# Another pace for expert tiles beside the last convolutions and the last mixing, and the last image's norms with both halves together

## The chip, the cores and the metric

The kernel runs on one core of a Trainium2 chip. The metric is the device time of one execution in microseconds, given as the median of three runs. A profiled execution of the same program is used to see where the time goes. Its engines are TensorE (PE, whose weight loads are listed apart as PEld), VectorE (DVE), ScalarE (ACT), GpSimd (POOL) and SyncE (SP, which here mostly issues DMA transfers).

## The reference

Four images of 256 channels and 32 x 32 positions pass through one layer: a token mixer with a residual, and then a mixture of experts with a residual. Cut to what matters here:

```python
def mixer(xs):                                   # xs: tokens of one image, 1024 x 256
    xn = layernorm(xs, norm_w, norm_b)
    xm = mamba_v(xn in 4 groups of 64 channels) + skip * xn       # selective scans
    g  = sigmoid(conv1d(conv1d(xm, qdw), qpw));  xg = g * xm
    R  = conv1d(conv1d(xg, rdw), rpw) + xg
    xm2 = conv1d(conv1d([xs, R], fdw), fpw) + xs                  # "convolutions"
    x_local  = conv1d(xm2, lc)
    x_global = mha(xm2)                                           # "attention"
    x_out = gelu(layernorm([x_local, x_global] @ fc_w.T + fc_b, lgn_w, lgn_b))
    xi = conv2d_depthwise_3x3(ln_hw(x_out), dwc)                  # "taps"
    return layernorm(xi, norm_w, norm_b) @ proj_w.T + proj_b      # "mixing" ends here

x = x + mixer(ln_c(x))
t = tokens(x);  xf = ln_t(t)
top_w, top_i = top_k(xf @ Wg + bg, 2);  w = softmax(top_w)        # "routing", 8 experts
for e in range(8):
    out += w_of_e * (gelu(xf @ W1[e] + b1[e]) @ W2[e] + b2[e])    # "expert tiles"
return t + out
```

Everything is float32. Each of the 4096 tokens goes to two experts of 256 x 1024 and 1024 x 256 weights.

## The kernel before

An image is held as two chunks of 128 channels by 1024 tokens, and most products and norms work on a half of 512 tokens at a time (`h` in the names). The images are staggered. While the selective scan of one image runs, pieces of its neighbours are put between its steps: convolutions, attention, mixing and routing of earlier images, and the first norm of later ones. After the last scan (image 3, `b == B - 1`) there is a tail of three stages and a fourth of tiles alone:

- the last convolutions (`convolutions(B - 1)`), beside which run the taps, the last norm, the projection and the routing of image 2 (`around(B - 2)`, `sent_off(B - 2)`);
- the last attention (`attention(B - 1)`);
- the last mixing: `joined(B - 1)` (output product `ao`, product `fc`, first norm `lgn`, gelu), `around(B - 1)` (norm over positions, then two times eight taps on DVE into `xi`), `sent_off(B - 1)` (mean, second norm `fin`, projection `pr`, then the routing in `experts.dispatch`);
- expert tiles alone, and the way back of the output.

**The experts.** `dispatch` computes gates (`gate`), places (`places`) and scatters each token's row by sixteen indirect DMAs on POOL's queue into `XS`, one region per expert. For the last image it also writes eight blank blocks behind the regions (`blank_ends`, L1457, issued from ACT's queue at L1450). A *tile* is 256 rows of one expert. There are 39, in three series of 8, 8 and 23. A series can start when enough images have been routed: `experts.series` (L1709) then makes on DVE a table of which tile belongs to which expert, and SP reads the table to address the loads. One tile loads two halves of W1 and two of W2 (512 KB each), two biases and its rows `xs` (L1786), and then runs, by the tile's instructions in their order:

- `xp` (L1832): four transposes of the rows on PE, copied by DVE to `xT`, and four small DVE operations;
- `h` 0 to 3 (L1855): four groups of matmuls, each with two gelus on ACT into `hs` (L1860);
- `y` (L1865): sixteen matmuls in four groups (k 0 to 3 and 4 to 7, for two row halves), which read `hs`; then `ys` on DVE (L1870, L1875) and two indirect DMAs on POOL that add into `Y`.

The next tile's loads, rows and `xp` are issued between the groups of the tile that runs.

**The order of the work** is written out by the program itself. Under `tc.manual_schedule` every engine executes its instructions in the order in which the Python code issues them. The pieces are generators; a `beat()` raises a tick, and a generator that yields `n` is resumed `n` ticks later. The tile generator (`tiles()`, L1148) yields `T["pace",]` after each of its eight groups of matmuls, or 1 if no pace is set. A pace above 1 spreads the groups of a tile over more steps of the other pieces, a pace below 1 packs them. `PACE` (L1273) holds a pace for each part of the last mixing, and `pace(b, ticks)` sets it, for the last image alone. There is none for the last convolutions. When these are done, `hold` stops the tiles at the next tile's start until two steps before the last attention ends.

**Norms.** `inverse_deviation` (L1000) makes the squares of a half on ACT, their mean over the channels on PE (`var`, L371), and the root as exp of -0.5 ln on ACT (`root`, L352); first for one half, then for the other. Then DVE multiplies both channel chunks. Gelu, sigmoid and the pair ln and exp belong to different tables of ACT; `loaded[0]` keeps track, and an ACT_TABLE_LOAD is issued at each change.

PSUM is one pool of eight banks (`ps`). Activations live in pools of tiles of 8, 4 and 2 KB per partition; the weights of the tiles reuse the buffers of the scan steps (`dts`, `dt`), enough for two tiles.

Of the kernel before, what the change touches and what calls it, by code (L numbers as in the profile page):

```python
# [72 lines left out]
def network(  # L73
# [29 lines left out]
    B = x.shape[0]  # L103
# [25 lines left out]
    eps5 = cpool.tile([P, 1], F32, name="eps5")  # L129
# [14 lines left out]
    with tc.tile_pool(name="w_conv", bufs=1) as wp, tc.tile_pool(  # L144
        name="act8", bufs=8
    ) as act8, tc.tile_pool(name="act4", bufs=7) as act4, tc.tile_pool(
        name="act2", bufs=17
    ) as act2, tc.tile_pool(name="steps", bufs=2) as actd, tc.tile_pool(
        name="steps4", bufs=6
    ) as acts, tc.tile_pool(name="rows", bufs=3) as actc, tc.tile_pool(  # L150
        name="small", bufs=1
# [190 lines left out]
        def half(h):  # L342
            return ts(h, HALF)
# [8 lines left out]
        def root(r, var, eps, scale=1.0):  # L352

            log_exp()
            nc.scalar.activation(r, var, AF.Ln, bias=eps, scale=scale)
            nc.scalar.activation(r, r, AF.Exp, scale=-0.5)
# [10 lines left out]
        def column_mean(name, chunks):  # L367

            out = ps(name)
            for ci, chunk in enumerate(chunks):  # L370
                nc.tensor.matmul(  # L371
                    out, ones_mean, chunk, start=(ci == 0), stop=(ci == len(chunks) - 1)
                )
            return out
# [110 lines left out]
        T = {}  # L485
# [511 lines left out]
            if b == B - 1:  # L997
                T["pace",] = ticks

        def inverse_deviation(name, xc):  # L1000
            r = a4(f"r_{name}")

            def squares(h):
                sq = [a2(f"sq_{name}_{h}_{c}") for c in range(NC2)]
                for c in range(NC2):
                    nc.scalar.activation(sq[c], xc[:, c, half(h)], AF.Square)
                return sq

            for h in range(2):
                sq = squares(h)  # L1010
                yield 1
                var = column_mean(f"var_{name}_{h}", sq)
                yield 2
                root(r[:, half(h)], var, eps5)
                yield 1
            yield 1
            for c in range(NC2):
                nc.vector.tensor_tensor(xc[:, c, :], xc[:, c, :], r, ALU.mult)
                yield 1

        def joined(b):

            xloc, oT = XLOC.pop(b), OT.pop(b)
            pace(b, PACE["product"])
            xglo = a8(f"xglo_{b}")
            T["attending", b] = True
            yield from in_turn(
                CO_H, lambda at: product(
                    f"ao_{b}_{at[0]}_{at[1]}", aoutT_s, at[0],
                    [oT[ci][:, half(at[1])] for ci in range(NC2)],  # L1030
                ),
                lambda at, r: nc.scalar.activation(
                    xglo[:, at[0], half(at[1])], r, AF.Identity, bias=ob[:, at[0] : at[0] + 1]
                ),
            )

            xc = XC[b] = a8(f"xc_{b}")
            both = (xloc, xglo)
            yield from in_turn(
                CO_H, lambda at: product(  # L1040
                    f"fc_{b}_{at[0]}_{at[1]}", fcT_s, at[0],
                    [both[ci // 2][:, ci % 2, half(at[1])] for ci in range(4)],
                ),
                lambda at, r: nc.scalar.activation(
                    xc[:, at[0], half(at[1])], r, AF.Identity, bias=fcb[:, at[0] : at[0] + 1]
                ),
            )

            T["joining", b] = True
            pace(b, PACE["norm"])  # L1050
            yield from inverse_deviation(f"lgn_{b}", xc)
            for c in range(NC2):
                nc.scalar.activation(
                    xc[:, c, :], xc[:, c, :], AF.Gelu, bias=col("lgn_b", c), scale=col("lgn_w", c)
                )
            loaded[0] = None
            log_exp()
            yield 2
# [44 lines left out]
        def sent_off(b):  # L1103

            xc = XC.pop(b)

            def centre(h, mean):
                for c in range(NC2):
                    nc.vector.tensor_tensor(
                        xc[:, c, half(h)], xc[:, c, half(h)], mean, ALU.subtract  # L1110
                    )

            pace(b, PACE["norm"])
            xr = a8(f"xr_{b}")
            nc.sync.dma_start(xr, x[b].rearrange("(c p) n -> p c n", p=P))
            yield from in_turn(
                range(2),
                lambda h: column_mean(f"mean_{b}_{h}", [xc[:, c, half(h)] for c in range(NC2)]),
                centre,
            )  # L1120
            yield from inverse_deviation(f"fin_{b}", xc)

            def residual(at, r):
                co, h = at
                inner = xr[:, co, half(h)]
                nc.vector.scalar_tensor_tensor(
                    inner, r, prb[:, co : co + 1], inner, ALU.add, ALU.add
                )

            yield from in_turn(  # L1130
                CO_H, lambda at: product(
                    f"pr_{b}_{at[0]}_{at[1]}", projT_s, at[0],
                    [xc[:, ci, half(at[1])] for ci in range(NC2)],
                ), residual,
            )
            pace(b, PACE["routing"])
            for ticks in experts.dispatch(
                b, xr, act8.tile(experts.XR, F32, tag="a8", name=f"XR_{b}"), root,
                log_exp,
            ):  # L1140
                if experts.counted == b:
                    pace(b, PACE["rows"])
                yield ticks
            T["sent", b] = True
            pace(b, 1)
# [118 lines left out]
        def until(*flag):  # L1264
            while not T.get(flag):
                beat()
# [3 lines left out]

        PARTS = 2 * NB

        PACE = {"product": 4, "norm": 2.2, "taps": 0.9, "routing": 2, "rows": 0.75}  # L1273
        with tc.manual_schedule(engines=ALL):
            log_exp()
            start(weights(), first_normalised())
            drain()
            first_part()
            for b in range(B):
                for p in range(PARTS):  # L1280
                    at = b * PARTS + p
                    stop = b > 0 and p == PARTS // 2 - 1 or at == len(parts) - 1
                    if b == 0 and p == 0:
                        start(later_weights())
                    if b == 0 and p == 2:
                        start(normalised(1))
                    if b > 0 and p == 0:
                        start(convolutions(b - 1))
                    if at == len(parts) - 1:
                        start(tiles())  # L1290
                    for i in range(NSTEP):
                        scan(at, i, stop)
                        if b > 0 and p == 0 and i == 9:
                            whole(b - 1)
                        beat()
                    if b > 0 and p == PARTS // 2 - 1:
                        drain()
                        start(
                            one_by_one(attention(b - 1), joined(b - 1)), finish_part(at),
                            one_by_one(  # L1300
                                local(b - 1), *([around(b - 2)] if b > 1 else []),
                                *([normalised(b + 1)] if 1 < b < B - 1 else []),
                            ),
                        )
                        if b > 1:
                            flag = "attending" if b == B - 1 else "joining"
                            start(behind_flag((flag, b - 1), sent_off(b - 2)))
                        if b == 1:
                            start(normalised(b + 1))
                        while not T.get(("attended", b - 1)):  # L1310
                            beat()
                        resume(at + 1)
            T["scanned",] = True
            start(
                flagged(finish_part(len(parts) - 1), "whole", B - 1),
                flagged(convolutions(B - 1), "convolved"),
                one_by_one(around(B - 2), sent_off(B - 2)),
            )
            until("convolved")
            T["hold",] = True  # L1320
            until("held")
            start(flagged(attention(B - 1), "attended", B - 1, 2), local(B - 1))
            until("attended", B - 1, 2)
            T["hold",] = False
            start(one_by_one(joined(B - 1), around(B - 1), sent_off(B - 1)))
            drain()

# [24 lines left out]
class Experts:  # L1352
# [11 lines left out]
    T = 256  # L1364
# [649 lines left out]
```

## Time and profile before

| | |
|---|---|
| three runs | 2481.73, 2473.77, 2473.78 us |
| median | 2473.78 us |
| profiled execution | 2480.27 us, of which the span from first to last instruction 2478.30 us |
| PE busy | 2131.6 us (86% of the span), 8810 matmuls |
| DVE busy | 1631.0 us (66%) |
| ACT busy | 1196.3 us (48%) |
| POOL busy | 1101.3 us (44%) |
| mean granted PE clock | 0.909 |
| DMA | 244.31 MB, mean 99 GB/s |

The busy shares are averages over the whole span. Up to about 1664 us the scans run, and DVE is busy for 1372 of these 1664 us; the tail behind it takes the remaining 815 us. In this part the page's row of the granted clock, in tenths over 40 slices, reads 7 to 9, and 9 in most slices of the tail.

Some ways of reading are needed later. In the timeline a line gives the start, the length from the first to the last of the merged instructions, engine, source line, operation, and in brackets the idle time before it with the instruction that ended it. PE counts each float32 matmul as two, so a group of four in the code is `x8` there. Matmuls overlap, so the difference of two starts, not the length, is the cost of a group. The granted clock is 1.00 where PE may run at full speed.

### The profile page before, as it was taken

The page shows a single profiled execution, that of the slowest core. Times are in us where ns is not written, and L with a number is a line of the kernel's source. Part 1 is how long each engine was busy: PE and PEld are TensorE (multiplying, and loading weights), DVE is VectorE, ACT ScalarE, POOL GpSimd, SP SyncE. Part 2 cuts the span into 40 slices and gives each one's busy share as a digit, 9 for nine tenths or more (in the row PEclk, how much of TensorE's full clock was granted, in tenths as well). Part 3 has the DMA queues.
Part 4 walks back from the last instruction along what each step waited for, and adds up shares of the span by engine and source line. Part 5 has one row for each costly group of instructions (what it writes and reads, how often), then busy time and mean ns, then how long its engine had stood idle before and what let it go on. Part 6 is the DMA issues. An engine that isn't in the chain of part 4 may idle for free. (4 is left out here: it accounts for less than half of the span.)

```text
span 2478.3 us, 28314 instructions
## 1 busy us (share of the span) xinstructions
PE 2131.6 (86%) x8810; PEld 947.8 (38%) x8810; DVE 1631.0 (66%) x2255; ACT 1196.3 (48%) x2020; POOL 1101.3 (44%) x1182
## 2 busy tenths in 40 slices
PE   7777768999978799987689999568999978899995
PEld 2111112322211132222113223115672456788885
DVE  3978998866898978789888787984425254211111
ACT  4554445568655448764264786324238542122221
POOL 0767776622676850465866115561131011322221
PEclk7978988999998899988788999779999988899998
DMA  3534343220343330133422102343330144666665
GB/s 89 140 96 107 95 103 80 58 57 26 77 100 98 74 74 26 35 104 91 124 61 59 46 22 69 88 147 105 112 109 16 58 134 133 194 196 191 195 198 156
DMA packets 154981, 244.31 MB, mean 99 GB/s; under 512 B 34184, under 2 KB 103452, under 8 KB 154816
## 3 DMA queue, kind: packets, MB, share of 16 engines
q1 hardware_dynamic: 135640, 217.05, 30.9%
q0 software_dynamic: 13264, 17.85, 3.7%
q10 hardware_dynamic: 5912, 7.45, 0.9%
q8 instruction: 74, 1.21, 0.2%
q14 instruction: 91, 0.75, 0.1%
HBM read 141.16 MB, written 33.98 MB: 71 GB/s over the span
## 5 line engine op out<-in xcount | busy, mean ns | idle before, releaser
L607 POOL TENSOR_TENSOR hs<-hs,cs 128x512 f32<-128x512 f32 x512 | 670.5, 1311 | 212.2 <-DVE hs L602 166.8
L613 PE MATMUL yp<-hs,quads 128*32 128x512 f32 x1024 | 345.8, 695 | 161.2 <-POOL hs L607 118.9
L588 ACT ACTIVATE dA<-dts,A 128x512 f32<-128x512 f32 x512 | 342.5, 713 | 277.6 <-DMA dts<-dt 189.8
L595 DVE TENSOR_TENSOR dBu<-dts,bs 128x512 f32<-128x512 f32 x512 | 347.7, 679 | 69.6 <-PE bs L580 17.6
L1881 POOL DMA_INDIRECT Y<-ys,dest x70 | 111.0, 1585 | 592.8 <-DVE ys L1875 586.4
L602 DVE TENSOR_TENSOR_SCAN hs<-dA,last,dBu 128x512 f32<-128x512 f32 x256 | 327.6, 1280 | 24.9 <-DVE dBu L595 0.5
L602 DVE TENSOR_TENSOR_SCAN hs<-dA,dBu 128x512 f32<-128x512 f32 x256 | 312.4, 1220 | 31.3 <-ACT dA L588 6.2
L1860 ACT ACTIVATE hs<-h,b 128x256 f32<-128x256 f32 x280 | 117.0, 471 | 398.8 <-PE h L1855 211.3
L928 ACT ACTIVATE e<-st 128x512 f32<-128x512 f32 x512 | 263.2, 606 | 84.8 <-PE st L918 84.5
L1865 PE MATMUL y<-w,hs 128*128 128x256 f32 x1120 | 270.2, 394 | 12.3 <-ACT hs L1860 12.3
L1855 PE MATMUL h<-xT,w 128*128 128x256 f32 x1120 | 254.4, 383 | 1.2 <-DVE xT L1833 1.2
L1865 PEld LDWEIGHTS y<-w,hs 128*128 128x128 f32 x1120 | 219.7, 199 | 55.0 <-ACT hs L1860 14.4
L1833 DVE COPY xT<-xp 128x512 f32<-128x512 f32 x35 | 24.2, 691 | 323.8 <-PE xp L1832 323.7
L606 POOL COPY last<-hs 128x1 f32<-128x1 f32 x256 | 66.9, 261 | 371.8 <-DVE hs L602 340.7
L1855 PEld LDWEIGHTS h<-xT,w 128*128 128x128 f32 x1120 | 214.1, 192 | 41.3 <-issue 10.7
L580 PE MATMUL bs<-u,xpwT_s 128*32 128x512 f32 x1024 | 177.9, 674 | 43.9 <-DVE hs L602 23.8
L613 PEld LDWEIGHTS yp<-hs,quads 128*32 128x32 f32 x1024 | 55.7, 119 | 414.2 <-POOL hs L607 280.8
L970 DVE TENSOR_TENSOR e<-e,e 128x512 f32<-128x512 f32 x256 | 171.2, 730 | 54.1 <-ACT e L928 29.9
L918 PE MATMUL st<-qk 32*128 32x512 f32 x1024 | 193.1, 653 | 6.8 <-DVE hs L602 4.5
L496 PE MATMUL up<-xn,inwk 64*128 64x512 f32 x256 | 138.8, 688 | 11.5 <-DVE hs L602 11.4
L960 PE MATMUL av<-e,v 128*32 128x512 f32 x1024 | 142.6, 621 | 0.0
L918 PEld LDWEIGHTS st<-qk 32*128 32x128 f32 x1024 | 67.6, 187 | 131.9 <-issue 87.6
(273 smaller groups left out, 2511.8 us busy)
## 6 DMA issues: line engine op xcount, KB each, us to landing
w<-in_W_dram SPq DMA_DIRECT2D x136, 512.0 KB
dts<-dt SPq DMA_DIRECT2D x512, 128.0 KB
cs<-cd SPq DMA_DIRECT2D x512, 64.0 KB
xs<-XS SPq DMA_DIRECT2D x35, 260.0 KB
b<-in_b_dram SPq DMA_DIRECT2D x35, 128.0 KB
xn<-in_x_dram SPq DMA_DIRECT2D x8, 512.0 KB
XL<-xl SPq DMA_DIRECT2D x8, 512.0 KB
xl<-XL SPq DMA_DIRECT2D x4, 1024.0 KB
```

The costliest lines, as they stand in the source:

```text
L580: nc.tensor.matmul(bs[r], xpwT_s[:, n, s : s + 1].to_broadcast([P, 32]), T[b, n, "u"][:, half(h)], start=True, stop=True,)
L588: nc.scalar.activation(dA, T[b, n, h, "dts", g][:, 0, :], AF.Exp, scale=A[:, g, n, q : q + 1])
L595: nc.vector.tensor_tensor(dBu, T[b, n, h, "dts", g][:, 1, :], T[b, n, h, "bs", q], ALU.mult)
L602: nc.vector.tensor_tensor_scan(hs, T[b, n, h, "dA", i], dBu, 0.0 if h == 0 else last, ALU.mult, ALU.add)
L607: nc.gpsimd.tensor_tensor(hs, hs, T[b, n, h, "cs", q], ALU.mult)
L613: nc.tensor.matmul(T[b, n, h, "yp"][ts(g, 32)], quads, T[b, n, h, "hs", q * GD + g], start=(q == 0), stop=(q == GS - 1),)
L918: nc.tensor.matmul(sts[i], k[r, ts(kt, P)], q[r, half(h)], start=True, stop=not shifted)
L928: nc.scalar.activation(es[i], sts[i], AF.Exp, scale=1.0 / HD**0.5)
L960: nc.tensor.matmul(accs[0][ts(i, HD)], v8[:, kt, ts(4 * g + i, HD)], es[i], start=(kt == 0), stop=(kt == NK - 1),)
L970: nc.vector.tensor_tensor(first[i], first[i], es[i], ALU.add)
L1855: nc.tensor.matmul(hp[:, i, :], w1(c, k), xT[:, c, :], start=(c == 0), stop=(c == NC2 - 1))
L1865: nc.tensor.matmul(yp[:, ts(t, C)], hs[:, k, ts(t, P)], w2(k), start=(k == 0), stop=(k == NHC - 1))
```

## The change

The paces are changed: all but `rows` become smaller, `rows` becomes larger, and the last convolutions get a pace of their own, which is taken back to 1 before `hold`. And for the last image alone (`b == B - 1`) both norms that go through `inverse_deviation` take the squares of both halves first, then both means over the channels, then both roots, with fewer steps between; for the other images the order stays.

```diff
-        def inverse_deviation(name, xc):
+        def inverse_deviation(name, xc, alone):
+
             r = a4(f"r_{name}")
...
-            for h in range(2):
-                sq = squares(h)
-                yield 1
-                var = column_mean(f"var_{name}_{h}", sq)
-                yield 2
-                root(r[:, half(h)], var, eps5)
-                yield 1
-            yield 1
+            if alone:
+                sq = [squares(h) for h in range(2)]
+                var = []
+                for h in range(2):
+                    yield 1
+                    var.append(column_mean(f"var_{name}_{h}", sq[h]))
+                for h in range(2):
+                    yield 1
+                    root(r[:, half(h)], var[h], eps5)
+            else:
+                for h in range(2):
+                    sq = squares(h)
+                    yield 1
+                    var = column_mean(f"var_{name}_{h}", sq)
+                    yield 2
+                    root(r[:, half(h)], var, eps5)
+                    yield 1
+                yield 1
             for c in range(NC2):
                 nc.vector.tensor_tensor(xc[:, c, :], xc[:, c, :], r, ALU.mult)
                 yield 1
...
-            yield from inverse_deviation(f"lgn_{b}", xc)
+            yield from inverse_deviation(f"lgn_{b}", xc, b == B - 1)
...
-            yield from inverse_deviation(f"fin_{b}", xc)
+            yield from inverse_deviation(f"fin_{b}", xc, b == B - 1)
...
-        PACE = {"product": 4, "norm": 2.2, "taps": 0.9, "routing": 2, "rows": 0.75}
+        PACE = {
+            "convolutions": 1.6, "product": 2, "norm": 1.2, "taps": 0.67, "routing": 1.3, "rows": 1
+        }
...
+            T["pace",] = PACE["convolutions"]
             until("convolved")
+            T["pace",] = 1
             T["hold",] = True
             until("held")
```

## The prediction

> **What bounds the kernel now.** I read the busy time by stage first, with the stage borders taken from TensorE's timeline: the last convolutions (image 3, beside routing of image 2), the last attention, the last mixing (output product, two norms, taps, routing of image 3), then tiles alone.
>
> ```profile
> core 0: us, PE busy (x) PEld busy (x) DVE busy (x) ACT busy (x) POOL busy (x), PEclk, DMA share, GB/s
> 1663.67:1853.93 190.26, 182.59 (x709) 126.15 (x709) 79.88 (x168) 71.36 (x115) 35.74 (x43) 0.97 0.38 117
> 1853.93:1941.64 87.71, 87.71 (x641) 25.86 (x640) 47.92 (x74) 73.35 (x145) 10.41 (x15) 1.00 0.06 13
> 1941.64:2180.64 239.00, 203.88 (x802) 156.45 (x801) 78.78 (x216) 76.76 (x137) 49.41 (x62) 0.89 0.49 146
> 2180.64:2440.73 260.09, 260.09 (x1241) 228.81 (x1240) 45.64 (x144) 60.45 (x144) 57.77 (x54) 1.00 0.63 179
> ```
>
> From 1663.67 on no other engine is busy for half of a stage, except ACT and DVE in attention: TensorE, which works strictly in its written order, sets the pace. What can be won there is its idle time and its lower clock: little in the convolutions (0.97), nothing in attention and among the tiles (1.00), most in the mixing (0.89). Next, who TensorE waited for, in the mixing and then in the convolutions (total, times, longest).
>
> ```profile
> PE y L1865 <- ACT hs L1860: 12.3, 4, 7.7
> PE xp L1832 <- DMA xs<-XS: 6.7, 1, 6.7
> PE mean L371 <- DVE xi L1097: 4.7, 1, 4.7
> PE var_fin L371 <- ACT sq_fin L1006: 4.1, 1, 4.1
> PE places L1567 <- DVE oh L1560: 3.3, 1, 3.3
> PE var_lgn L371 <- ACT sq_lgn L1006: 2.6, 1, 2.6
> PE pr L362 <- DVE xi L1018: 1.5, 1, 1.5
> ```
>
> ```profile
> PE var_fin L371 <- ACT sq_fin L1006: 4.8, 2, 3.7
> PE mean L371 <- DVE xi L1097: 1.7, 1, 1.7
> PE h L1855 <- DVE xT L1833: 1.2, 1, 1.2
> ```
>
> So 35.1 us idle in the mixing and 7.7 in the convolutions. Two of the mixing's waits in the timeline: the eight blank-row transfers hold ACT's queue, and the table of the third series comes late for tile 16's rows.
>
> ```profile
> 2099.61 10.24 ACTq L1450 DMA_DIRECT2D XS<-blank  x8
> 2110.43 3.78 PE L1865 MATMUL y<-w,hs 128*128 128x256 f32 x8 [7.73 <-ACT hs L1860]
> ...
> 2153.86 0.18 DVE L1701 TENSOR_SCALAR table<-first 128x23 int32<-128x23 f32 x1
> 2158.52 0.38 SPq L1786 DMA_DIRECT2D xs<-XS  x1
> 2164.91 1.11 PE L1832 MATMUL xp<-ident,xs 128*128 128x128 f32 x4 [6.68 <-DMA xs<-XS]
> 2180.64 0.60 PE L1832 MATMUL xp<-ident,xs 128*128 128x128 f32 x4
> 2194.89 0.60 PE L1832 MATMUL xp<-ident,xs 128*128 128x128 f32 x4
> ```
>
> The last two lines give the unit: undisturbed, a tile takes 14.25 us of TensorE (xp 0.44, four h of 1.73, two y of 3.46).
>
> **The work that stands still.** Full-speed times from timeline starts: rp, pr, mean, var, ao, qkp and vp 1.72 for each product, fp and fc 3.44, qd 10.7 together, gp 3.8, raw 1.7, gate 3.4, places 0.4. Convolutions: 75.2 us of these and 7 tiles with the next xp (100.2), sum 175.4; measured 190.3, so 14.9 lost (7.7 waits, 7.2 low clock). Mixing to tile 17's xp: 43.4 (ao 6.9, fc 13.7, var_lgn 3.4, mean 3.4, var_fin 3.4, pr 6.9, raw, gate, places 5.5) and 138.6 of tiles 7 to 16, sum 182.0; measured 239.0, so 57.0 lost (35.1 waits, 21.9 low clock).
>
> **What the change moves.** In the issue order of the built kernels the last convolutions hold 7 tiles and the next xp before, 5 and an xp after; nine tiles, 7 to 15, begin their gelus in the mixing before, eleven, 5 to 15, after. Two tiles, 28.5 us of TensorE, change stage. Each takes along four 512 KB weight loads, two bias loads and a row load on SP's queue, and two scatter-adds on POOL's. The mixing's traffic becomes (146 x 239 + 2 x 2.55 MB) / 250 us = 160 GB/s, where 2.55 MB is 179 GB/s over 14.25 us; the stage of tiles alone carries 179 without a wait, so I price this at nothing (unhidden, a row load would cost the 6.7 of tile 16). As the work only moves, the time changes by the change in the losses.
>
> **Convolutions, after.** I went along TensorE's new order with the durations of the rows, starting at 1663.67. (1) Clock and first wait: 4.1 us (as now). (2) The mean of image 2 now stands behind only one tile's h: TensorE is there at 1685.9, the sixteen taps end near 1691.3 (now 1692.7, less the 1.4 us of the second tile's xT on DVE): 5.4 wait and 2.4 low clock, the latter as after the mixing's 4.65 us wait; 7.8. Bounds: 1.7 (today's wait, if a tile step lies ahead) and 12. (3) var_fin of the second half, one h behind the first: ACT still has sigmoid, three table loads of 1.28, a root and one d: 3.5 wait and 2.7 low clock, as today's 3.7 cost; 6.2. (The flag `alone` is off for image 2.) (4) First rp behind DVE's taps: under 1. After it fp, vp and qkp find their inputs done (the second d4r taps end at 1754.9, needed at 1755.9). Sum about 18.2, that is +3.3.
>
> **Mixing, after**, clock from attention's end, now's loss then after's. var_lgn: 4.4 (wait 2.6) to 0: both halves' squares are ready at 32.4, TensorE comes at 33.2. The first tile in the norm: 7.8 to 11.1. Here ACT's order becomes gelu h0, table, root, table, gelu h1, table, root, table, gelu h2, two big gelus, two tables, gelu h3: six loads of 1.28, two roots of 1.35, 2.4 of big gelus; h3's gelu ends at 56.6, while y wants it at 47.9. Behind it wait tile 7's xp, the second bn on DVE and so the taps. Bounds 7.8 and 15.5 (the whole stretch from h0's gelu to h3's). Tile 8's rows: 0 to 8.0. Before, the second series' table was made during attention; now on DVE behind tile 6's ys, ready at 69.4. From tile 16's rows: 4.7 to the row load's issue, 6.4 to landing: 80.5, TensorE is there at 74.1. Bounds 0 (other row loads are not waited for) and 8.2. Mean: 7.3 to 4.6 (DVE's last three taps behind tile 9's xT). var_fin: 5.9 to 2.9. pr: 1.8 to 0.7. The y behind 32 gate matmuls took 6.3 for 3.5: 3.5 to 0, as the gate is now split round an h (that order in the convolutions shows 3.7). places: 6.1 to 3.6. Blank rows: 10.9 (wait 7.7) to 0: they now stand behind gelu h3, and 14 us of y, xp, y and h cover the 10.2; without cover 7.7 again. Tile 16's rows: 8.2 to 8.7, its table still stands behind tile 14. After's sum 39.6, that is 17.4 less.
>
> Sum: 3.3 - 17.4 = **-14.1 us**. The profiled execution took 2480.27 (span 2478.30 and 1.97 around it) and would take 2466.2; it lies 6.5 above the median of 2473.78, so the forecast for the median is 2473.8 - 14.1 = **2460**.
>
> A rule that speaks against it: the Trainium skill, ScalarE: Activation LUTs, "What ACT_TABLE_LOAD costs", adds about 1.38 us of drain to each load of 1.28. By it the six loads would put 8.3 us more on the first tile, and the sum would be -5.8. Here the instruction behind a load starts 0.01 to 0.02 us after its 1.28 (1707.58 to 1708.87), so the row decides.
>
> On the low clock: TensorE: Matmul & The Clock Gate, Part 1, wants about 3.4 us of idleness before half clock. Here matmuls were slower already after 2.60 us (var_lgn 2.36 for 1.72). By the rule the waits of 2.3 (var_fin) and 2.2 (places) would cost no clock, the sum -16.
>
> **Rivals.** *Both new waits are covered* (0.28): tile 8's rows land in time and the first tile loses only today's 7.8: -14.1 - 8.0 - 3.3 = -25.4, 2448. For: no row load but tile 16's was ever waited for. Against: tile 8's table now has just tile 16's place. *The work moves and the losses stay* (0.05): the mixing loses 57 as before, +3.3, 2477. For: dependences of the norms are a chain, more matmuls between only delay it. Against: the blank rows and the var_lgn wait change place in the order itself. *Slower* (0.09): in the mixing none of the old waits goes and the two new ones come on top: ACT's queue, where roots and tables of the norm alternate with the tile's gelus, holds each y: 57 + 11.1 + 8.0 = 76.1 lost, +22.4, 2496. It decides once the mixing loses over 66 us (57.0 - 3.3 + 12.4). For: 12.3 of today's waits are of this kind. Against: 7.7 of them are the blank rows'. That the change misses its counts is excluded by the issue order: eleven tiles, 5 to 15, begin their gelus in the mixing.
>
> **How the numbers follow.** 0.5%, 12.4 us, is about what a measurement of this kernel can tell from no change: below 2461.4 is faster. The forecast case has 0.58, its own range 2453 to 2466 (tile 8's and the first tile's bounds by halves); nearly three quarters of it, 0.42, I put below 2461.4, since the clock after each wait was taken at its dear end. Faster: 0.42 + 0.28 = 0.70; same: 0.16 + 0.05 = 0.21; slower: 0.09. Range: low 2447, the covered case; high 2474, the forecast plus 4 for the first tile at its bound, 4 for the mean at its bound and 6 for old mixing waits that stay; outside are the slower case, 2477 and a tail of the covered case, about 0.2.
>
> **What would show it.** Right: attention starts 25 us earlier (near 1829); tile 17's xp comes about 250 us after attention's end, 239 now; mixing clock about 0.93; new lines "xp waits for xs" twice, and "y waits for hs" without the 7.7. Wrong: a convolution stage over 172 us, a mixing over 258, or waits in the tiles-only stage.

## The result and the profile after

| | before | after |
|---|---|---|
| first comparison, four runs each | 2475.35 us | 2477.34 us, ratio 1.0002 [0.9981, 1.0023] |
| second comparison, 18 and 10 runs | 2480.67 us | 2471.69 us, ratio 0.9964 [0.9949, 0.9978] |
| profiled execution (span) | 2480.27 (2478.30) us | 2474.80 (2472.8) us |

No change by the forecast's bound of 0.5%; the second comparison shows a gain of 9.0 us, 0.36%, with an interval from 0.22% to 0.51%. The forecast was 2460 and faster by 14.1 us.

The profile shows why the runs spread. Between the start and the first `xp` behind the scans, TensorE's order is the same in both kernels, yet this point stands at 1663.67 us before, at 1665.74 after, and at 1658.08 in a second profiled execution of the changed program. So a kernel is compared here by its **tail**: from that `xp` to the reduction behind the last tile. It took 777.06 us before, 769.64 and 770.07 in the two executions after: 7.0 to 7.4 us less.

Busy time by stage, changed kernel (convolutions, attention, mixing to tile 17's `xp`, tiles alone; columns as before):

```profile
core 0: us, PE busy (x) PEld busy (x) DVE busy (x) ACT busy (x) POOL busy (x), PEclk, DMA share, GB/s
1665.74:1831.17 165.43, 156.89 (x574) 102.91 (x573) 75.30 (x152) 63.94 (x98) 35.27 (x47) 0.94 0.36 109
1831.17:1921.61 90.44, 89.35 (x642) 25.99 (x641) 47.94 (x74) 73.30 (x145) 5.13 (x6) 0.98 0.08 23
1921.61:2175.29 253.68, 223.66 (x938) 176.69 (x937) 84.46 (x232) 83.29 (x153) 55.66 (x68) 0.93 0.50 149
2175.29:2435.38 260.09, 260.09 (x1242) 228.83 (x1240) 45.65 (x144) 60.33 (x144) 57.98 (x54) 1.00 0.63 179
```

The two tiles, 28.5 us, went from the first row to the third as forecast: 190.3 became 165.4, 239.0 became 253.7. The last stage is the same to the hundredth. Attention, in which nothing was edited, took 90.4 for 87.7. The waits of TensorE in the mixing (total, times, longest); lines of the changed file stand up to 15 lower than before:

```profile
PE xp L1847 <- DMA xs<-XS: 12.6, 2, 6.7
PE y L1880 <- ACT hs L1875: 6.9, 2, 3.6
PE xp L1847 <- issue: 4.9, 1, 4.9
PE mean L371 <- DVE xi L1108: 2.5, 1, 2.5
PE places L1582 <- DVE ex L1577: 1.7, 1, 1.7
PE var_fin L371 <- ACT sq_fin L1007: 1.4, 1, 1.4
```

Together 30.0 us, for 35.1 before. The first line is tile 8's and tile 16's rows, the second the first tile in the norm; both were forecast. The third was not: it is tile 14's `xp`.

### The profile page after: what moved, and what is told of

Same layout as the page of the kernel before. It is cut to its first block, busy times and chain, and to the rows that moved or that the text cites. A ratio compares the mean times of both kernels' runs of the same rounds, so it can differ in the third digit from the quotient of the medians.

```text
span 2472.8 us, 28317 instructions
## 1 busy us (share of the span) xinstructions
PE 2134.3 (86%) x8810; PEld 947.7 (38%) x8810; DVE 1632.3 (66%) x2255; ACT 1194.4 (48%) x2019; POOL 1101.3 (45%) x1182
## 5 line engine op out<-in xcount | busy, mean ns | idle before, releaser
L1870 PEld LDWEIGHTS h<-xT,w 128*128 128x128 f32 x1120 | 213.2, 191 | 38.9 <-issue 8.4
L580 PE MATMUL bs<-u,xpwT_s 128*32 128x512 f32 x1024 | 184.9, 692 | 42.9 <-DVE hs L602 23.5
```

The costliest lines, as they stand in the source:

```text
L580: nc.tensor.matmul(bs[r], xpwT_s[:, n, s : s + 1].to_broadcast([P, 32]), T[b, n, "u"][:, half(h)], start=True, stop=True,)
L1870: nc.tensor.matmul(hp[:, i, :], w1(c, k), xT[:, c, :], start=(c == 0), stop=(c == NC2 - 1))
```

## The experiments

Losses below are the stage's length less the full-speed work of the forecast (convolutions 175.4 with seven tiles, 146.9 with five; mixing 182.0 with ten tiles, 210.5 with twelve). All kernels compute the whole result. "Median" of a kernel with a single run is that run.

| kernel | convolutions | attention | mixing | its loss | tail | median, ratio |
|---|---|---|---|---|---|---|
| before | 190.3 | 87.7 | 239.0 | 57.0 | 777.1 | |
| changed | 165.4 | 90.4 | 253.7 | 43.2 | 769.6 | 2477.3, 1.000 |
| changed, again | 165.3 | 90.4 | 254.4 | 43.9 | 770.1 | 2471.7, 0.996 |
| conv_only | 165.3 | 88.7 | 266.2 | 55.7 | 780.3 | 2489.6, 1.0044 [1.0027, 1.0061] |
| norm_only | 190.2 | 88.0 | 210.7 | 28.7 | 749.0 | 2447.9, 0.987 [0.985, 0.989] |
| mixing_only | 190.3 | 88.0 | 220.3 | 38.3 | 758.6 | 2463.7, 0.993 [0.991, 0.996] |
| paces_only | 165.4 | 87.7 | 249.4 | 38.9 | 762.6 | 2466.5 |
| blank_pool | 165.4 | 87.7 | 246.6 | 36.1 | 759.8 | 2469.4 |
| table1 | 165.4 | 89.4 | 244.5 | 34.0 | 759.4 | 2462.5 |
| table2 | 169.0 | 87.7 | 238.6 | 28.1 | 755.5 | 2461.7 |
| product4 | 165.3 | 87.7 | 252.9 | 42.4 | 766.0 | 2462.2 |
| roots | 165.3 | 87.7 | 249.6 | 39.1 | 762.7 | 2466.0 |
| all_four | 165.5 | 89.4 | 227.8 | 17.3 | 742.7 | 2450.8, 0.9885 [0.986, 0.991] |
| norm_table2 | 190.2 | 87.7 | 197.6 | 15.6 | 735.5 | 2438.4, 0.984 [0.982, 0.987] |
| before_p5 | 190.2 | 88.1 | 230.2 | 48.2 | 768.7 | 2468.0 |
| norm_p2 | 190.2 | 88.1 | 227.7 | 45.7 | 766.1 | 2460.6 |
| norm_p5_table2 | 190.2 | 88.1 | 210.3 | 28.3 | 748.8 | 2448.8, 0.988 [0.986, 0.991] |

The stage of tiles alone was 260.1 in all of them. The scans ended anywhere from 1655.1 us (norm_p2) to 1669.3 (blank_pool), 14 us apart, with the same order of TensorE up to there. Single runs therefore tell little here, and the tails tell more. Only the changed kernel was profiled twice, though: its stages repeat within 0.7 us, while stages of the same written order differ from kernel to kernel by up to 2.7 us (attention) and 3.6 us (the convolutions of table2). A tail that differs by less than 4 us proves little by itself.

### The changed kernel again, and its parts

> The changed kernel once more, nothing edited, to see which part of the tail's gain is real. From the two profiles on hand: convolutions 190.3 to 165.4 us, attention 87.7 to 90.4, mixing up to tile 17's transposes 239.0 to 253.7, together 7.4 less; the scans before them 2.1 more although their instructions are the same; medians 2.0 more. Theory A (the tail's gain is real, the scans differ from execution to execution by several us): the same four tail stages within 1 us here, the scans' end anywhere from 1662 to 1672, and over five rounds a ratio of 0.996 to 0.999. Theory B (the tail varies as well and the gain of 7.4 is chance): tail stages that differ by over 3 us from those of the first profile, ratio 0.999 to 1.002.

Theory A: convolutions, attention and mixing repeat within 0.7 us, the scans do not (they end at 1658.1, outside A's 1662 to 1672). The ratio, 0.9964, lies in the range that A gave. The tail's gain of 7.0 to 7.4 us is real, and it is half of the forecast.

The first part alone:

```diff
-        PACE = {"product": 4, ...
+        PACE = {"convolutions": 1.6, "product": 4, ...
...
+            T["pace",] = PACE["convolutions"]
             until("convolved")
+            T["pace",] = 1
```

> The kernel before with one edit: the pace of 1.6 for the last convolutions, set back to 1 before the hold; norms and the paces of the mixing as before. Five tiles instead of seven beside the convolutions, so two tiles (28.5 us) go to the stage of tiles alone. Theory A (losses add up by their places): convolutions 165.4 us as in the changed kernel, attention 90.4 (the DVE of the tile just before it is still at work), the mixing 239 plus 8 for tile 8's rows, whose table is now made in the mixing, less up to 8 for tile 16's rows, which leave it; total 2 to 14 us slower than before. Theory B (the convolutions' new order costs nothing of its own): convolutions 162, mixing 239, total within 2 us of before.

The sum fits A (ratio 1.0044, tail 3.2 longer), its places do not: tile 8's rows were not waited for, while the mean waited 10.0 us. Holding the tiles back earns nothing of its own.

The norms alone (the new `inverse_deviation`, all paces old):

> The changed kernel's norms (squares, variances and roots of both halves together) with all paces of the kernel before. Theory A: the wait for the squares of lgn (4.4 us with its clock) goes and a wait of the first tile behind the alternating tables comes, as far as the old pace of 2.2 lays tile groups between the roots; fewer steps in each norm also mean fewer tile groups in the mixing, so about one tile fewer there; net -4 to +4 us. Theory B (the norms' order is what helps in the changed kernel): mixing's loss per tile falls, total 6 us or more faster.

28.1 us off the tail, ratio 0.987: A's size fails, and B's "6 us or more" is met more than four times over. This is the largest effect of any part, and the changed kernel has only a quarter of it, so B's other half, that the norms' order is what helps there, is not shown.

The new norms and mixing paces without the convolutions' pace:

> The changed kernel without the pace of the last convolutions: new norms and new mixing paces, seven tiles beside the convolutions as before, so tiles 7 to 17 beside the mixing. Theory A: convolutions 190.3, attention 87.7, the second series' table made in attention again, so no wait for tile 8's rows (8.5 us with its clock); the third series' table meets the mixing as before; total 5 to 12 us faster than before. Theory B (holding tiles back beside the convolutions is what pays): no faster than before.

18.4 us off the tail, more than A gave, so B falls: holding the tiles back is not what pays. Here tile 16's rows were waited for 14.9 us, and there was still more gain than in the changed kernel.

The new paces with the old norms:

> The changed kernel with its norms in the old order, all new paces kept. With the old paces the new norms alone took 28 us off the tail (777.1 to 749.0), and with them the new paces of the mixing put 9.7 back and the convolutions' pace 11.0 more. Theory A (the norms gain by having no tile's gelu between the roots, so three fewer table loads; at a pace of 1.2 gelus stand there anyway): the norms are worth under 10 us among the new paces, tail 766 to 780. Theory B (the effects add): tail about 798, norms worth 28 here too.

762.6: B, that the effects add, is off by 35 us; A's direction holds, and even its lower end was too high. The tail is 7.3 us shorter than the changed kernel's. Of these, 2.7 are attention's (87.7 here), which runs ahead of the edit and can't be the norms' doing. But the mixing is 4.3 shorter too, so the norms that gain 28 us alone **cost** something among the new paces: tile 14's rows are not waited for at all, and var_lgn (4.5 us) and tile 15's rows (2.2) take a part of that back.

### Each wait by itself

**Tile 14's rows.** Two of SP's waits in the changed kernel around this load (2098 to 2126 us), and the timeline of ACT's queue, SP and TensorE there:

```profile
SPq L1801 <- DMA w<-in_W_dram: 2.8, 1, 2.8
SPq L1832 <- DMA XS<-blank: 1.1, 1, 1.1
```

```profile
2099.78 11.65 ACTq L1465 DMA_DIRECT2D XS<-blank  x8
```

```profile
2106.05 1.25 SPq L1829 DMA_DIRECT2D w<-in_W_dram  x2
...
2109.48 0.34 SPq L1832 DMA_DIRECT2D b<-in_vecs_dram  x1
2113.20 0.38 SPq L1801 DMA_DIRECT2D xs<-XS  x1
```

```profile
2113.13 3.62 PE L1880 MATMUL y<-w,hs 128*128 128x256 f32 x16
2121.62 1.12 PE L1847 MATMUL xp<-ident,xs 128*128 128x128 f32 x4 [4.87 <-issue]
```

A row load waits for a weight load, and a bias load for a blank row, though none reads the other's data. In the trace the transfers of SP and of ACT signal their landing by one of the same eight semaphores (numbers 100 to 107), which the built program deals out in turn, and one that takes a semaphore first waits until its last user has landed, as SP's two waits show: the row load takes 103, as the weight load at 2106.05 had, and the bias load 101, as the blank row at 2102.60 had. POOL's transfers use eight others (109 to 116). A tile issues seven loads, so its row load normally follows the bias load of the tile before, long landed. The eight blanks on ACT's queue take places in the turn; then tile 14's row load meets tile 14's own second-half weights, issued at 2106.05.

```diff
-        ins = self.nc.scalar.dma_start(
+        ins = (queue or self.nc.scalar).dma_start(
...
-                    ends[0:1, e, :], engines=[mybir.EngineType.Activation], min_val=0,
+                    ends[0:1, e, :], engines=[mybir.EngineType.Pool], min_val=0,
...
-                )
+                ),
+                nc.gpsimd,
             )
```

> The changed kernel with one edit: the eight blank-row transfers are issued from POOL's queue instead of ACT's. The tail, from its first tile transposes to the reduction at its end, took 769.6 and 770.1 us in two executions of the changed kernel; tile 14's transposes waited 4.9 and 5.7 us there, 7.0 with the low clock behind it. Its row load was issued at 2113.20, the blanks sat on ACT's queue from 2099.78 to 2111.43. Theory A (the row load waits because the blanks took places in the rotation of completion semaphores that the hardware queues of SP and ACT share; it now waits for a weight load of the same tile that left only 6 us before): without blanks in that rotation tile 14's wait goes, tail 763. Theory B (the blanks' bytes hold the DMA engines): the same bytes still move, tile 14 or 15 still waits 3 us or more, tail 768 to 774. By either, POOL's scatters end some 10 us later, and tile 16's rows, now waited for 6.7 to 8.0 us, may come later still.

With the blanks on POOL's queue the row load left earlier and the wait all but went (the mixing started 0.7 us later here, at 1922.33):

```profile
2107.75 0.61 SPq L1833 DMA_DIRECT2D b<-in_vecs_dram  x1
2110.39 0.38 SPq L1802 DMA_DIRECT2D xs<-XS  x1
```

```profile
2117.42 0.66 PE L1848 MATMUL xp<-ident,xs 128*128 128x128 f32 x4 [0.64 <-DMA xs<-XS]
```

The mixing is 7.1 us shorter (7.0 expected), so the blanks' place on ACT's queue is the cause. (The tail, 759.8 for A's 763, also holds the 2.7 us of attention.) Counted from the mixing's start the row load left 188.1 us in, against 191.6: 3.5 us, and SP's two waits for strangers are 3.9. From issue to `xp` it is 7.0 us here and 8.4 in the changed kernel; whether this 1.4 is the blanks' bytes was not tried. B, that bytes alone hold the load, does not fit: they still moved, and the wait was 0.6.

**Tile 8's rows.**

```diff
-                if i == 0:
+                if len(tables) == s:
                     tables.append(experts.series(s, temp))
...
                 while T.get(("hold",)):
-                    T["held",] = True
+                    if not T.get(("held",)):
+                        T["held",] = True
+                        yield 6
+                        tables.append(experts.series(1, temp))
                     yield 1
```

> The changed kernel with one edit: the table of the second series is made during the last attention (six ticks after the hold), as the order of the kernel before had it, instead of inside the mixing. Theory A (tile 8's rows are late only because of the table): the wait of 6.0 to 6.6 us at tile 8's transposes goes, 8.5 with its clock, attention stays at 90.4, tail 761.5. Theory B (something else is late at that place, the row load's turn on SP or a buffer): tile 8 or 9 still waits 3 us or more, tail 766 or more. Theory C: the table's twenty or so DVE operations in attention delay TensorE there, attention 92 or more.

Theory A: the wait is gone and the mixing 9.2 us shorter. Attention took 89.4, under A's 90.4, but C holds at a smaller size: the start of attention is undisturbed here, and the 1.6 us over 87.7 are lost where the table is made. DVE works on the table until 1845.6, starts its products `e` behind it, and TensorE's group of `av` at 1846.46 takes 2.68 us, for 1.04 at that place in blank_pool.

**Tile 16's rows.**

```diff
-                if i == 0:
+                if len(tables) == s:
...
                     ahead(n + 1, at)
+                    if order[n][0] == 1 and len(tables) == 2 and experts.counted == B - 1:
+                        tables.append(experts.series(2, temp))
                     yield T.get(("pace",), 1)
```

> The changed kernel with one edit: the table of the third series is made right after the last image's places are counted, beside tile 13 or 14, instead of during tile 15. Theory A (tile 16's rows wait for the table): the wait of 6.7 to 8.0 us goes, 8.9 to 10 with its clock, tail 760. Theory B (they wait for the sixteen scatters of the last image, whose last leaves POOL at 2135.6, and for the weight buffers of tile 14, free at 2141.8): the row load leaves at 2143 at the earliest and lands at 2149.5 against a need at 2152.1, so at most 1 us of wait is left; if the scatters land over 5 us after they are issued, 2 to 4 us stay, tail 763 to 767.

The wait is gone, so neither the scatters nor the buffers were behind it. The mixing fell by 15.1 us, not 8.9: tile 14's wait went to 0.7 as well. The blanks are still on ACT's queue, but they start 4.0 us later (2103.80; 2.3 us later when counted from the mixing's start), and tile 14's row load left at 2110.41, 187.1 us into the mixing for 191.6; y waited 1.8 us behind the blanks. The convolutions, not edited, took 3.6 us more in this execution.

**The first tile in the norm.** ACT's timeline of the changed kernel, from the squares to the small root:

```profile
1951.73 2.18 ACT L1007 ACTIVATE sq_lgn<-xc 128x512 f32<-128x512 f32 x4
1961.92 0.84 ACT L1875 ACTIVATE hs<-h,b 128x256 f32<-128x256 f32 x2 [8.02 <-PE h L1870]
1962.78 1.28 ACT L349 ACT_TABLE_LOAD   x1
1964.07 0.69 ACT L355 ACTIVATE r_lgn<-var_lgn,eps 128x512 f32<-128x512 f32 x1
...
1965.44 1.28 ACT L1875 ACT_TABLE_LOAD   x1
1966.74 0.84 ACT L1875 ACTIVATE hs<-h,b 128x256 f32<-128x256 f32 x2
1967.59 1.28 ACT L349 ACT_TABLE_LOAD   x1
...
1977.24 0.84 ACT L1875 ACTIVATE hs<-h,b 128x256 f32<-128x256 f32 x2
```

The same stretch of norm_only:

```profile
1969.21 2.20 ACT L1007 ACTIVATE sq_lgn<-xc 128x512 f32<-128x512 f32 x4
1971.42 1.28 ACT L349 ACT_TABLE_LOAD   x1
1972.78 0.69 ACT L355 ACTIVATE r_lgn<-var_lgn,eps 128x512 f32<-128x512 f32 x1
...
1978.43 1.28 ACT L1064 ACT_TABLE_LOAD   x1
1979.76 1.24 ACT L1064 ACTIVATE xc<-xc,V 128x1024 f32<-128x1024 f32 x1
...
1985.48 1.28 ACT L1871 ACT_TABLE_LOAD   x1
1986.77 0.84 ACT L1871 ACTIVATE hs<-h,b 128x256 f32<-128x256 f32 x2
```

In norm_only no gelu of a tile stands between the squares and the small root; TensorE runs the y of a tile whose gelus are done. In the changed kernel, four groups of h fall into this stretch, and the last of their gelus ends at 1978.1, though TensorE had ended the four groups of h by 1966.9. Two edits move the gelus out of there: the products' pace back to 4, and both roots in one step.

```diff
-            "convolutions": 1.6, "product": 2, "norm": 1.2, ...
+            "convolutions": 1.6, "product": 4, "norm": 1.2, ...
```

> The changed kernel with one number put back: the pace of the products 4 instead of 2. In the issue order this moves the four gelus of tile 6 out from between the two roots of the first norm: ACT then runs table, both roots, table, both big gelus, table, table, four gelus of a tile, table, the small root, as against the changed kernel's gelu, table, root, table, gelu, table, root, table, gelu, big gelus, table, table, gelu, table, small root. Theory A (the first norm's tile is what the changed kernel pays there): its two waits of y for gelus, 6.9 us and 10.5 with clock, fall under 3, tail 760 to 764 as against 769.6 and 770.1. Theory B (the 28 us of the norms alone lie elsewhere, in the second norm or the routing): y still waits 5 us or more in the norm, tail 767 or more.

```profile
PE xp L1847 <- DMA xs<-XS: 17.1, 2, 9.4
PE y L1880 <- ACT hs L1875: 6.3, 1, 6.3
PE pr L362 <- DVE xi L1029: 4.6, 1, 4.6
PE var_lgn L371 <- ACT sq_lgn L1007: 2.6, 1, 2.6
```

These are the mixing's waits of product4. The norm's two waits of y are gone, as A said. But the sum is 30.6 us, against 30.0: the one wait of y that is there now is the blanks' again, at 2089.87, tile 8 waits 9.4 instead of 6.0, and pr and var_lgn wait again. The mixing fell by 0.8 us, the rest of the tail's 3.6 is attention. A's size and B both miss: the wait was removed and paid elsewhere.

```diff
-                for h in range(2):
-                    yield 1
-                    root(r[:, half(h)], var[h], eps5)
+                yield 1
+                for h in range(2):
+                    root(r[:, half(h)], var[h], eps5)
+                yield 1
```

> The changed kernel with the two roots of a half issued in one step, so that no gelu can stand between them; gelus may still stand before the first and between the big gelus. Theory A (each gelu between roots costs a pair of table loads on the way to y): one pair less, 2.6 us, and gelu 1 waits for both roots: the y waits fall from 6.9 to about 4.3, tail 765 to 767.5. Theory B (the wait is set by DVE's products with the root or by the bn behind the big gelus): y's waits stay within 1 us, tail 769 to 770.5.

The waits of y fell from 6.9 to 5.0 and the mixing by 4.1 us; the tail's 762.7 is lower than A's range, again by attention's 2.7. The order of groups is otherwise that of the changed kernel, and no other wait in the mixing moved by over 0.5 us. All waits together fell by only 0.8 us (30.0 to 29.2); most of the 4.1 is clock, 1.5 of it at the mean, by a chance that is told below.

### Removing waits together

> The changed kernel with four edits together: blanks from POOL's queue, the second and the third series' tables made early, both roots in one step. Alone the first three took 10.3, 10.5 and 14.4 us off the tail of 769.9, but all three numbers hold 1 to 3 us of attention's start, and those of the first and third both hold tile 14's wait of 7. Theory A (each wait is its own): mixing 253.7 - 7.0 (tile 14) - 8.5 (tile 8) - 8.9 (tile 16) - 2.6 (roots) = 226.7, attention 87.7, tail 740, some 30 us faster than the changed kernel. Theory B (one wait gone uncovers the next): tail 748 or more.

> The new norms with the old paces, and the third series' table made right after the last image's places are counted. The norms alone gave a tail of 749.0 us and 2447.9 us (ratio 0.987). Theory A (tile 16's rows wait for the table here as well, 6.9 us, 9 with clock): tail 740, ratio 0.982 to 0.985. Theory B (the scatters of the last image land later than the row load wants them in this order): the wait stays over 4 us, tail 745 to 749, ratio 0.985 to 0.989.

all_four: A's mixing, 226.7, was measured as 227.8, and the ratio is 0.9885; the tail is 742.7 for A's 740, since attention took 89.4, as in table1, and not 87.7. norm_table2 beats all others; its stages and the mixing's waits:

```profile
1662.82:1853.01 190.19, 182.57 (x710) 126.42 (x709) 79.95 (x168) 71.32 (x115) 35.64 (x43) 0.97 0.40 115
1853.01:1940.70 87.69, 87.69 (x641) 25.86 (x640) 47.94 (x74) 73.30 (x145) 10.40 (x15) 1.00 0.06 13
1940.70:2138.26 197.56, 186.77 (x802) 146.03 (x802) 78.82 (x216) 74.44 (x135) 49.19 (x62) 0.98 0.60 176
```

```profile
PE mean L371 <- DVE xi L1108: 5.0, 1, 5.0
PE var_lgn L371 <- ACT sq_lgn L1007: 2.6, 1, 2.6
PE h L1868 <- DVE xT L1846: 2.4, 1, 2.4
PE places L1580 <- DVE ex L1575: 0.8, 1, 0.8
```

The mixing's clock is 0.98 for 0.89 before, its waits 10.8 us for 35.1. A's tail of 740 is undercut by 4.5: with the wait for rows, two short ones beside the blanks (0.9 and 1.0 in norm_only) went too.

### Own order, or a shift

Two kernels shift the tile groups by the products' pace alone: before with 5, and norm_only with 2. A third does so with the best one.

> The kernel before with one number changed: the pace of the products 5 instead of 4; norms in their old order. In the issue order this shifts which tile groups meet the norms: behind both roots of lgn come table, one big gelu, two tables, one gelu, as against gelu, big gelu, two tables, gelu before, and no gelu stands among the roots of the second norm. Theory A (the 28 us of the new norms alone come mostly from the shift, since a norm with fewer steps moves all tile groups behind it): a shift without new norms gains a good part too, tail 750 to 767 against 777.1. Theory B (they come from the norms' own order): tail 772 to 782.

> The new norms with the old paces, but for the pace of the products, 2 instead of 4. Roots of lgn still without a gelu between them; behind them gelu, big gelu, two tables, two gelus, table, small root, table, where norms alone had big gelus, table, small root, table. Theory A (shift): the waits of y for gelus come back and others change place, tail 756 to 770 against 749.0. Theory B (the norms' own order): tail 746 to 753.

> New norms, old paces but the products' 5, and the third series' table made early (tail 735.5 with the products' 4). No gelu stands from the squares of lgn to the first xz, so the taps start some 1 to 2 us earlier against TensorE's order, whose groups there are fewer. Theory A: the waits at the mean (5.0, 8.2 with clock) and at var_lgn (2.6) stay within 2 us, tail 732 to 739. Theory B (each shift deals the waits anew): a wait appears that norms alone did not have (y for gelus, pr, places or rows over 3 us), tail 740 to 752.

before_p5 gains 8.4 us with the old norms, between the two ranges: more than B allows, less than A gave. norm_p2 loses 17.1 of the norms' 28.1, as A said. norm_p5_table2 loses 13.2 against norm_table2 (B): y waits 8.6 us for gelus behind the blanks, where norm_table2 has no such wait. The same y stands behind the blanks in before (7.7), conv_only (7.0), mixing_only (6.0), product4 (6.3), before_p5 (7.8) and norm_p2 (8.1), and hardly in norm_only (0.9). So a good part of what the norms gain alone seems to be where they put the groups behind them, the blanks' wait above all. How much is left for their own order can't be told from these runs: with each pace it would have to be measured anew.

## Why the prediction was wrong

**The account by losses held for the terms that it had.** Convolutions: loss 18.5 for 18.2 forecast, the mean's wait 4.4 for 5.4, var_fin's 2.6 for 3.5, rp's 0.4. Attention starts 24.8 us earlier when counted from the scans' end (forecast 25). The mixing's clock is 0.93, as said.

**Mixing, term by term** (wait and low clock, from TensorE's starts): first tile in the norm 10.6 for 11.1; tile 8's rows 8.5 for 8.0; mean 4.2 for 4.6; var_fin 1.7 for 2.9; pr 0 for 0.7; gate 0.2 for 0; places 2.0 for 3.6; tile 16's rows 8.9 for 8.7. These sum to 36.1 against 39.6: a little cheaper than said, since I took the clock's dear end. table1, table2 and product4 each took one of the three large waits away, and roots shortened one. Two things in this part of the forecast were wrong without deciding it. Its terms for the kernel before add up to 55.9, and it set after's sum against the measured 57.0; term by term the mixing falls by 16.3 and not 17.4. And the second series' table was not made during attention before: DVE finished it at 1948.08, 6.4 us into the mixing, early enough for tile 8's rows (1990.13 in the changed kernel, 68.5 us in, for 69.4 forecast).

**The step that failed: "Blank rows: 10.9 (wait 7.7) to 0".** It was priced on ACT's queue alone, by the gelus behind the blanks, and there it was right: y no longer waits for them. The blanks (11.65 us in the changed kernel) also stand in the turn of the loads' semaphores, and tile 14's row load was late by that: 7.0 us with clock instead of 0. blank_pool shows it. The price of 6.7 for an unhidden row load stood in the text, and was set to nothing because the traffic fits; but the load lost 3.5 us before it was issued, behind semaphores. Whether traffic had a part in the other 1.4 is open.

**The second miss: attention was taken as unchanged.** It took 2.7 us more in both executions of the changed program, and 87.7 in blank_pool, table2, product4, roots and paces_only, which have the same tiles around it (88.7 in conv_only, where `ys` was late as well; 89.4 in table1 and all_four, where the table is made within it). Its start in the changed kernel and in blank_pool:

```profile
1831.17 1.99 PE L918 MATMUL st<-qk 32*128 32x512 f32 x14
1833.50 0.69 DVE L1885 TENSOR_TENSOR ys<-y,b 128x512 f32<-128x512 f32 x1 [3.11 <-PE st L918]
1834.25 1.12 PE L918 MATMUL st<-qk 32*128 32x512 f32 x2 [1.09 <-DVE ys L1885]
```

```profile
1834.62 2.00 PE L918 MATMUL st<-qk 32*128 32x512 f32 x16
1834.73 0.69 DVE L1886 TENSOR_TENSOR ys<-y,b 128x512 f32<-128x512 f32 x1 [2.16 <-PE y L1881]
```

In blank_pool `ys` starts 0.1 us after the first `st` is recorded, in the changed kernel 2.3 us after it; two `st` then wait for the bank that `ys` reads, and a low clock follows (0.50 from 1836 to 1838 us). Why `ys` starts late is open.

Together: -14.1, +7.0 (tile 14), +2.7 (attention), +0.3 (convolutions: their loss grew by 3.6, not 3.3), -3.5 (the mixing's other terms) gives -7.6, and the tails of the first profiles of both kernels show -7.4.

**The base** was off too. The 14.1 us were taken from 2473.78, the median of three runs; 18 later runs of the same kernel have 2480.67. The forecast gain lay only 1.7 us beyond the bound for "faster", and either miss alone was enough to bring it back.

**The rivals.** Both waits covered (2448): no, tile 8's rows and the first tile cost what the main case said. Losses stay (57): no, 43. Slower: no, the mixing lost 43.2, and its point was 66. A rival was missing: that parts of the change work against each other. The norms' gain was counted as two terms, var_lgn and the first tile; as runs show it is 28 us alone and less than nothing among the new paces.

**The table load and the clock.** In the stretch above, the root behind a load starts at 1964.07, 0.01 after 1962.78 + 1.28, so the row decided rightly over ScalarE: Activation LUTs of the Trainium skill (section "What ACT_TABLE_LOAD costs"). On the clock, the length of a wait does not settle its cost. The mean's wait in the two executions of the changed kernel:

```profile
2023.62 2.08 PE L371 MATMUL mean<-xi,ones_mean 128*128 128x512 f32 x2 [2.47 <-DVE xi L1108]
```

```profile
2016.07 1.12 PE L371 MATMUL mean<-xi,ones_mean 128*128 128x512 f32 x2 [2.48 <-DVE xi L1108]
```

The first cost another 1.6 us in slower matmuls (granted clock 0.50 from 2023.6 to 2025.6), the second 0.1 (1.00 from 2016 to 2018). blank_pool paid as the first did; roots, table1, table2 and all_four as the second, so about 1.5 us of what their mixing gained against the first execution is this chance. TensorE: Matmul & The Clock Gate of the Trainium skill (Part 1) puts the fall of the clock at about 3.4 us of idleness; here it fell after 2.47 in one execution.

## What to carry to other kernels

Where one engine works in a written order and helpers are interleaved by counted steps, an edit of any count deals the waits behind it anew; so measure each part alone and in pairs before adding prices, and prefer edits that take a wait's cause away (the tables made earlier, blanks off the shared queue) over edits that move work past it. For a DMA that is moved, look at the loads that share its completion semaphores, not only at its queue and its bytes. And when executions differ by more than the effect, compare the stage that the edit touches, by the same two instructions in each profile.

## What the hardware showed unexpectedly

- The scans of TensorE's same order ended between 1655.1 and 1669.3 us in the profiled executions, and 7.7 us apart in two executions of one program; in these two the stages of the tail repeat within 0.7 us.
- At the start of attention VectorE's `ys` comes 2 us late behind TensorE's work in both executions of the changed program and in conv_only, and not in the seven others that have five tiles beside the convolutions; the records show no cause.
- One and the same wait of TensorE, 2.47 us long, was followed by half clock in one execution and by full clock in another of the same program.
